# Two float products become PE transposes in the second layer of a graph network

## The chip, the cores and the metric

The kernel runs on one core of a Trainium2 chip. The metric is the device time of one execution in microseconds (us); lower is better. Before the change it is 5334.88 us, the median of three runs (5333.9 to 5344.31).

A core has five engines, each with its own queue that it works through in order: TensorE (PE, matrix products; its weight loads are listed apart as PEld), VectorE (DVE), ScalarE (ACT), GpSimd (POOL) and SyncE (SP, which only issues transfers here). They wait for each other by semaphores.

## The reference

Two layers of a graph network with 12,500 nodes, 200,000 edges sorted by destination, 64 features and 8 edge types, each layer followed by a residual and a layer norm. The change lies in the second one:

```python
Z = jnp.einsum('ni,rio->nro', h, fc_weight)
z_s = Z[src, etype]
z_d = Z[dst, etype]
aw = attn_weight[etype, :, 0]
e = jax.nn.relu(jnp.sum(jnp.concatenate([z_s, z_d], axis=1) * aw, axis=1))
m = jax.ops.segment_max(e, dst, num_segments=N)
ex = jnp.exp(e - m[dst])
denom = jax.ops.segment_sum(ex, dst, num_segments=N)
h_out = jax.ops.segment_sum((ex / denom[dst])[:, None] * z_s, dst, num_segments=N)
```

So it is a softmax over the edges that enter a node: a score per edge, the maximum over each destination's edges, the exponential of the difference, and a weighted sum.

## The kernel before

Edges are taken in runs of 512 (four chunks of 128), and two runs make a group: 391 runs, 196 groups. The edges being sorted, the destinations of a run fall into a window of W = 96 nodes. Work on a window is done with one-hot matrices: `oh` (edges by window places) and `ohT` (the other way round).

The second layer's function `sum1` handles one group. It is a Python generator that is cut into pieces by `yield`. The loop that calls it interleaves pieces of up to five groups in a fixed order, written out by hand (`group(i + 3)`, `node(i)`, `group(i)` and so on), and every engine's queue is filled in that order. The function `finish1` does the same for the nodes that are complete, from group 90 on. Going through `sum1`:

- Loads: SP brings `row` (L507) and `dw` (L606); POOL gathers the rows `zg` of the table of Z by eight indirect transfers a group (L95), into one of five buffers.
- `ps_row` (PE, L615) spreads the destinations' places over 96 partitions, ACT makes `ohT` of it (L616, L619), and PE looks up the destination's part of the score (`pq`, L624).
- DVE builds `oh` (L361), the scores (L630 to L640), and the largest score of each lane for each window place, `t` (L648 to L652).
- PE turns `t` with a transpose into `tt` (L658, tile pt), so that the window's places lie on partitions. DVE reduces it to one maximum a place, `m` (L663).
- L665: `m` lies on partitions and is wanted along the free axis, on all C = 65 partitions. It is a product with `m`, broadcast to 65 columns, as the stationary operand and the unit matrix as the moving one. The result is `rows`.
- DVE takes the larger of that and of the running maxima `top` (`most`, L673), and the difference `d` (L674); ACT writes `top` back (L675).
- L683: one row of `most` is turned back, so that the places lie on partitions again: a product of that row as the stationary operand with a 1 by 1 tile that holds a one. The result is `column`, one column a run.
- DVE splits `column` into three bfloat16 parts `mq` (`parts`, L434 to L437), PE looks up each edge's maximum from them (`pm`, L690), and DVE subtracts it from the score (`em`, L694 and L695).
- ACT takes the exponentials (L696, L698) and weighs the gathered rows (`wz`, L700). PE adds them up by window (`sums`, L704), and DVE adds the sums to the accumulators `acc` (L708, L709).

In PE's queue a steady group's order is: L704 (8 products), L683 (2), L615, L624 (8), L615, the transpose of a finished node L724, L658 (2), L690 (8), L665 (2). In DVE's queue it is: m, em, acc, most and d, the scores, t, mq, oh, each for the group whose turn it is.

The first layer (`sum0`, `finish0`) has the same manner of queues. Its products are L407 and L422, and it is not touched by the change.

Of the kernel before, what the change touches and what calls it, by code (L numbers as in the profile page):

```python
# [53 lines left out]
W = 96  # L54
# [11 lines left out]
C = D + 1  # L66
# [4 lines left out]
def gnn_kernel(ctx: ExitStack, tc, x, xT, xP, src, dstp, dst, et, eaT, u, W1, b1, W2, b2, fc, aw, out):  # L71
    nc = tc.nc
# [40 lines left out]
    with (  # L113
# [35 lines left out]
        ident = consts.tile([128, 128], F32, name="ident")  # L149
# [22 lines left out]
        one_f = consts.tile([1, 1], F32, name="one_f")  # L172
# [429 lines left out]
    def sum1(work, psum, n, chunks, idx, rel_of, et_of, row_of, wins_of, odd=0):  # L602
# [19 lines left out]
        for k in range(n * KS):  # L622
            s, i = divmod(k, KS)
# [32 lines left out]
        rows = pt[:C, n * EC:].rearrange("p (s w) -> p s w", s=n)  # L656
# [5 lines left out]
        m = work.tile([W, n], F32, name="m")  # L662
        nc.vector.tensor_reduce(m, tt, AX.X, OP.max)  # L663
        for s in range(n):
            nc.tensor.matmul(rows[:, s, :], m[:, s:s + 1].to_broadcast([W, C]), ident[:W, :W],  # L665
                             start=True, stop=True)
        yield

        most = work.tile([C, n, W], F32, name="most")
# [10 lines left out]
        column = pb[:W, 2 * n * W:2 * n * W + n]  # L680
        pm = pb[:, 2 * n * W + n:].rearrange("p (k j) -> p k j", j=3)
        for s in range(n):
            nc.tensor.matmul(column[:, s:s + 1], most[0:1, s, :], one_f, start=True, stop=True)  # L683
        yield
        mq = work.tile([W, n, 3], BF16, name="mq")
        parts(work, column, lambda i: mq[:, :, i], [W, n])
# [1 line left out]
        for k in range(n * KS):  # L688
            s, i = divmod(k, KS)
# [12 lines left out]
        for k in range(n * KS):  # L702
            s, i = divmod(k, KS)
# [48 lines left out]
    with (  # L752
# [14 lines left out]
        for i in range(-3, NG - 2):  # L767
            g = i + 3
            if g < NG:
                n, chunks, c = span(g)  # L770
                groups[g] = sum1(work, psum, n, chunks, row_i[:, c], rel[:, c], et_i[:, c],
                                 row_load(work, g), wins_load(g), g % 2)
# [53 lines left out]
    with tc.For_i(0, some):  # L826
# [21 lines left out]
        with (  # L848
            tc.tile_pool(name="r1", bufs=1) as work,
            tc.tile_pool(name="r1_ps", bufs=1, space=PSUM) as psum,  # L850
        ):
            acc, top = sums_of(work)

            def edges1(r, w):
                idx, rl, row, base = further(work, r, w)
                chunks = ds(r * KS, KS)
                etx = work.tile([EC, KS], I32, name="x_et")
                nc.vector.tensor_copy(etx, et_i[:, chunks])
                nc.vector.tensor_copy(idx, row_i[:, chunks])
                all_of(sum1(work, psum, 1, KS, idx, rl, etx, lambda: row, lambda engine: [base]))  # L860

            def node1(at):
                y = work.tile([P, 1, D], F32, name="y1")
                mv = work.tile([P, 1, nc.vector.BN_AGGR_DIM], F32, name="ln_mv")
                all_of(finish1(work, psum, lambda engine: at, lambda: (y[:, 0, :], mv[:, 0, :])))
                all_of(scale1(work, [at], y, mv))

            anew(edges1, node1)
# [45 lines left out]
```

## Time and profile before

| | us |
|---|---|
| median of three runs | 5334.88 |
| the profiled execution | 5314.15 |
| its span (first to last instruction) | 5312.4 |
| PE busy (matmuls) | 2942.6 (55%) |
| PE weight loads busy | 2299.9 (43%) |
| DVE busy | 2485.7 (47%) |
| ACT busy | 1445.6 (27%) |
| POOL busy | 2953.5 (56%) |

The profile is of one execution. An entry names the line, the engine, the operation, and the tiles as out<-in. In a table of groups there follow the count, the busy time in us, the mean time of one in ns, and the engine's idle time just before, with what ended it. The times at which matmuls end are modelled; when a result really arrived is seen from the instruction that waited for it. Busy times of an engine can overlap and say nothing on their own about what sets the end. The chain of waits goes back from the last instruction, at each step to what released it; where it finds no instruction that did, it says "another core or an unknown queue". The second layer fills the stretch from about 2640 us to the end.

### The profile page before, as it was taken

The page shows a single profiled execution, that of the slowest core. Times are in us where ns is not written, and L with a number is a line of the kernel's source. Part 1 is how long each engine was busy: PE and PEld are TensorE (multiplying, and loading weights), DVE is VectorE, ACT ScalarE, POOL GpSimd, SP SyncE. Part 2 cuts the span into 40 slices and gives each one's busy share as a digit, 9 for nine tenths or more (in the row PEclk, how much of TensorE's full clock was granted, in tenths as well). Part 3 has the DMA queues.
Part 4 walks back from the last instruction along what each step waited for, and adds up shares of the span by engine and source line. Part 5 has one row for each costly group of instructions (what it writes and reads, how often), then busy time and mean ns, then how long its engine had stood idle before and what let it go on. Part 6 is the DMA issues. An engine that isn't in the chain of part 4 may idle for free.

```text
span 5312.4 us, 62590 instructions
## 1 busy us (share of the span) xinstructions
PE 2942.6 (55%) x16633; PEld 2299.9 (43%) x16634; DVE 2485.7 (47%) x8113; ACT 1445.6 (27%) x3717; POOL 2953.5 (56%) x3140
## 2 busy tenths in 40 slices
PE   3455555555677777777454454445444455545454
PEld 2344444444555555555333333333333333333333
DVE  2022222222444444445455555555556556666566
ACT  1000000000111111111343343444444445444454
POOL 5466665566565565664255555555555555555553
PEclk6555555555556565656655555555555555555555
DMA  3121111111222222222111111111111111111111
GB/s 123 30 63 37 35 37 35 36 37 36 56 64 61 64 64 61 64 62 66 44 22 21 22 22 21 22 22 21 23 23 24 26 25 26 26 24 26 25 25 20
DMA packets 294054, 204.87 MB, mean 39 GB/s; under 512 B 214573, under 2 KB 214703, under 8 KB 293274
## 3 DMA queue, kind: packets, MB, share of 16 engines
q0 software_dynamic: 100032, 103.43, 9.8%
q1 hardware_dynamic: 189180, 87.46, 6.4%
q10 hardware_dynamic: 4480, 9.91, 0.6%
q8 instruction: 134, 2.20, 0.2%
q14 instruction: 228, 1.87, 0.1%
HBM read 158.55 MB, written 41.97 MB: 38 GB/s over the span
## 4 chain that ended last, share of the span: by engine, by line
another core or an unknown queue 32%; DVE 24%; PE 16%; issue 15%; ACT 9%; DVEq 2%; DMA 1%; POOL 0%; ACTq 0%; SPq 0%; POOLq 0%
PE pa L422 5%; ACT wz L700 4%; PE pm L407 3%; DVE oh L361 3%; DVEq L335 2%; PE pb L704 2%; DVE psc L648 2%; DVE oe L648 2%; DVE d L674 1%; DVE most L673 1%; PE pt L665 1%; DVE msg L416 1%; DVE t L651 1%; DVE psc L650 1%
## 5 line engine op out<-in xcount | busy, mean ns | idle before, releaser
L95 POOL DMA_INDIRECT zg<-z_tab,row_i x1563 | 1474.5, 943 | 1287.2 <-ACT top L675 641.5
L95 POOL DMA_INDIRECT bg<-b_tab,src_i x1523 | 1438.1, 944 | 1008.7 <-issue 398.4
L704 PE MATMUL pb<-oh,wz 128*65 128x96 f32 x3128 | 551.2, 368 | 553.7 <-ACT wz L700 304.4
L422 PE MATMUL pa<-oh,msg 128*64 128x96 f32 x3128 | 539.6, 364 | 574.3 <-ACT msg L417 441.4
L704 PEld LDWEIGHTS pb<-oh,wz 128*65 128x65 f32 x3128 | 494.6, 227 | 609.9 <-ACT wz L700 343.1
L422 PEld LDWEIGHTS pa<-oh,msg 128*64 128x64 f32 x3128 | 483.0, 222 | 600.7 <-ACT msg L417 454.2
L417 ACT ACTIVATE msg<-msg 128x512 f32<-128x512 f32 x191 | 120.0, 629 | 2089.5 <-DVE msg L416 1946.8
L407 PEld LDWEIGHTS pm<-aw,cb 128*128 128x128 f32 x3128 | 579.2, 284 | 135.8 <-issue 131.7
L407 PE MATMUL pm<-aw,cb 128*128 128x64 f32 x3128 | 618.6, 376 | 2.3 <-issue 2.3
L428 DVE TENSOR_TENSOR xa<-xa,pa 64x96 f32 x391 | 100.9, 258 | 817.7 <-remote 514.1
L416 DVE TENSOR_TENSOR msg<-pm,bg 128x512 f32<-128x512 f32 x191 | 131.4, 688 | 740.9 <-remote 608.8
L616 ACT ACTIVATE off<-ps_row,minus_p 96x512 bf16<-96x512 f32 x391 | 266.0, 680 | 553.4 <-remote 275.1
L615 PE MATMUL ps_row<-row,ones_row 1*96 1x512 bf16 x391 | 217.0, 555 | 340.6 <-ACT off L616 165.5
L700 ACT ACTIVATE wz<-zg,wz 128x64 f32<-128x64 f32 x1564 | 394.7, 335 | 6.4
L361 DVE TENSOR_TENSOR oh<-psc,rel 128x768 f32<-128x768 f32 x392 | 371.4, 948 | 7.0 <-DMA z_tab<-z 4.2
L665 PE MATMUL pt<-ident,m 96*65 96x96 f32 x782 | 176.5, 379 | 342.9 <-issue 145.9
L665 PEld LDWEIGHTS pt<-ident,m 96*65 96x65 f32 x782 | 119.5, 220 | 360.3 <-issue 151.5
L694 DVE TENSOR_REDUCE em<-pb 128x8 f32<-128x24 f32 x196 | 35.3, 180 | 509.9 <-remote 444.2
L696 ACT ACTIVATE pb<-d 65x192 f32<-65x192 f32 x196 | 64.2, 327 | 717.8 <-DVE em L694 443.0
L402 DVE TENSOR_SCALAR cb<-ps_row,iota_p 96x1024 f32<-96x1024 f32 x196 | 246.2, 1256 | 11.2 <-PE ps_row L355 7.2
L481 PE MATMUL pw<-wsd,x1T 64*125 64x16 f32 x212 | 60.9, 365 | 315.1 <-DVE y L454 314.5
L481 PEld LDWEIGHTS pw<-wsd,x1T 64*125 64x125 f32 x212 | 50.7, 295 | 377.1 <-DVE y L454 376.2
(151 smaller groups left out, 3982.0 us busy)
## 6 DMA issues: line engine op xcount, KB each, us to landing
z_tab<-z SPq DMA_DIRECT2D x106, 253.9 KB
zg<-z_tab,row_i POOLq DMA_INDIRECT x1563
cb<-in_eaT SPq DMA_DIRECT2D x195, 128.0 KB
bg<-b_tab,src_i POOLq DMA_INDIRECT x1523
aw<-a_tab SPq DMA_DIRECT2D x391, 24.0 KB
dw<-d_tab SPq DMA_DIRECT2D x391, 4.7 KB
row<-rel_tab SPq DMA_DIRECT2D x390, 2.0 KB
xn<-in_x SPq DMA_DIRECT2D x106, 31.2 KB
```

The costliest lines, as they stand in the source:

```text
L95: nc.gpsimd.indirect_dma_start(out=to[:, k, :], out_offset=None, in_=table[:, :], in_offset=bass.IndirectOffsetOnAxis(ap=idx[:, k:k + 1], ...
L361: nc.vector.tensor_tensor(oh, iota_n[:, None, :].to_broadcast([EC, n * KS, W]), rel_of.unsqueeze(2).to_broadcast([EC, n * KS, W]), OP.is_e ...
L402: nc.vector.tensor_scalar(cb[:W, :, :], ps_row, iota_p[:W], None, OP.is_equal)
L407: nc.tensor.matmul(pm[:, k, :], cb[:, s, i * EC:(i + 1) * EC], aw_t[:, s, :], start=True, stop=not raw)
L416: nc.vector.tensor_add(msg, pm, bg)
L422: nc.tensor.matmul(pa[D:, s, :], msg[:, k, :], oh[:, k, :], start=(i == 0), stop=(i == KS - 1))
L615: nc.tensor.matmul(ps_row[:, :RE], ones_row, row[:, s, :], start=True, stop=True)
L616: nc.scalar.activation(off[:, s, :], ps_row[:, :RE], AF.Abs, bias=minus_p[:W])
L648: nc.vector.tensor_mul(to, by_run[:, :, i, :], es[:, :, i].unsqueeze(3).to_broadcast([EC, n, half, W]))
L665: nc.tensor.matmul(rows[:, s, :], m[:, s:s + 1].to_broadcast([W, C]), ident[:W, :W], start=True, stop=True)
L700: nc.scalar.activation(wz[:, k, :D], zg[:, k, :D], AF.Copy, scale=wz[:, k, D:])
L704: nc.tensor.matmul(sums[:, s, :], wz[:, k, :], oh[:, k, :], start=(i == 0), stop=(i == KS - 1))
```

## The change

Two statements of `sum1` are changed. In both, the product of two float32 operands becomes the transpose operation of PE, with the same operands in the same roles: what is turned is the stationary operand, and the unit matrix (or the one) is the moving one. No instruction changes its place in a queue, and no buffer or loop is altered.

```diff
         for s in range(n):
-            nc.tensor.matmul(rows[:, s, :], m[:, s:s + 1].to_broadcast([W, C]), ident[:W, :W],
-                             start=True, stop=True)
+            nc.tensor.transpose(rows[:, s, :], m[:, s:s + 1].to_broadcast([W, C]), ident[:W, :W])
...
         for s in range(n):
-            nc.tensor.matmul(column[:, s:s + 1], most[0:1, s, :], one_f, start=True, stop=True)
+            nc.tensor.transpose(column[:, s:s + 1], most[0:1, s, :], one_f)
```

## The prediction

> **What bounds the kernel now.** The change touches the second layer alone, so I first looked at where that layer's time goes. The page's chain of waits comes first (shares of the span, by engine and by line).
>
> ```profile
> another core or an unknown queue 32%; DVE 24%; PE 16%; issue 15%; ACT 9%; DVEq 2%; DMA 1%; POOL 0%; ACTq 0%; SPq 0%; POOLq 0%
> PE pa L422 5%; ACT wz L700 4%; PE pm L407 3%; DVE oh L361 3%; DVEq L335 2%; PE pb L704 2%; DVE psc L648 2%; DVE oe L648 2%; DVE d L674 1%; DVE most L673 1%; PE pt L665 1%; DVE msg L416 1%; DVE t L651 1%; DVE psc L650 1%
> ```
>
> No engine carries the span. A third of the chain has no named owner, PE has 16% of it, and of the two lines that the change edits only L665 is listed, with 1%. The sums by stretch for the second layer (two windows, 2600 us; columns: length, then busy us of PE, PEld, DVE, ACT, POOL with their counts, then granted clock, DMA share, GB/s) show a stage bound by latency:
>
> ```profile
> 2640.00:3890.00 1250.00, 616.81 (x4114) 462.88 (x4115) 699.91 (x2439) 505.20 (x1405) 697.20 (x739) 0.54 0.12 22
> 3890.00:5240.00 1350.00, 668.95 (x4332) 502.97 (x4331) 812.29 (x3026) 644.11 (x1729) 729.18 (x773) 0.53 0.13 25
> ```
>
> DVE leads with 58% (1512 of 2600), PE has 49%. Taking the starts of L694 as the beat, the 196 groups come 13.3 us apart in the first 90 and 14.0 us apart while nodes are finished too. The last groups, for which nothing is gathered any more, show the beat that the same arithmetic can keep (timeline; columns: start, duration, engine, line, operation, tiles, and in brackets the idle time before):
>
> ```profile
> 5264.79 0.17 DVE L694 TENSOR_REDUCE em<-pb 128x8 f32<-128x24 f32 x1
> ...
> 5266.15 0.24 DVE L673 TENSOR_TENSOR most<-top,pt 65x96 f32<-65x96 f32 x1
> ...
> 5268.65 0.80 PE L683 MATMUL pb<-one_f,most 1*96 1x1 f32 x4
> ...
> 5273.71 0.17 DVE L694 TENSOR_REDUCE em<-pb 128x8 f32<-128x24 f32 x1
> ```
>
> From em to em: 8.92 us. There DVE has no idle time in front of m, em and most, and L683 comes as soon as DVE has made most. L665, started at 5264.92, is done at 5265.82, before most wants it. A group with gathers in flight looks different:
>
> ```profile
> 4050.09 0.40 PE L690 MATMUL pb<-mq,ohT 96*128 96x3 bf16 x8
> 4050.81 0.90 PE L665 MATMUL pt<-ident,m 96*65 96x96 f32 x4 [0.32 <-issue]
> ...
> 4052.43 0.18 DVE L694 TENSOR_REDUCE em<-pb 128x8 f32<-128x24 f32 x1 [1.67 <-PE pt L665]
> ...
> 4055.32 0.25 DVE L673 TENSOR_TENSOR most<-top,pt 65x96 f32<-65x96 f32 x1 [1.43 <-PE pb L704]
> ```
>
> em needs L690, whose drawn end is 4050.49, and starts 1.9 us after it; most needs L665, whose drawn end is 4051.71, and starts 3.6 us after it. So PE's results arrive later than drawn while POOL gathers, and this lateness (510 us of DVE idle before L694, 208 us before L663) is the bulk of the 32% without an owner. The page's names for it are not to be trusted: em doesn't read L665's result, and most doesn't read L704's.
>
> **The change part by part.** On every engine the order of instructions stays the same; only the kind of four matmuls in a group changes. The rows that price it:
>
> ```profile
> L665 PE MATMUL pt<-ident,m 96*65 96x96 f32 x782 | 176.5, 379 | 342.9 <-issue 145.9 <-DVE m L663 123.8 <-DVE oh L361 73.0
> L683 PE MATMUL pb<-one_f,most 1*96 1x1 f32 x782 | 151.8, 290 | 22.5 <-issue 10.8 <-DVE most L673 4.4 <-DVE ln_shift L746 2.2
> L658 PE MATMUL pt<-ident,t 128*96 128x128 f32 x391 | 117.7, 401 | 121.9 <-DVE mq L434 63.8 <-issue 37.1 <-DVE t L652 8.1
> ```
>
> There are 391 runs of edges, and each has one L665, one L683 and one L658. The float products leave 782 records, two for each product, with two weight loads; the transpose of L658 leaves 391, one each. That is the whole mechanism: a float product goes through the array in two recorded passes, a transpose in one.
>
> *Step 1, L665's size.* Four records take 0.90 us a group (176.5/196): the first about 0.42, each further one 0.16 later. Two take about 0.42 + 0.16 = 0.58, near the 0.60 (117.7/196) of L658, which is the larger shape. Saving 0.32 us.
>
> *Step 2, L683's size.* Four records take 0.775 us (151.8/196), so two take 0.29 + 0.17 = 0.46. Saving 0.32 us. Both together: 0.64 x 196 = 125 us of PE's time, 782 matmuls and 782 weight loads fewer. That is the ceiling if every bit lay on the path.
>
> *Step 3, what of L683 is on the path.* Its result is read by L434. In the group without gathers L683 ends at 5269.45 and L434 comes at 5271.86, with DVE busy between: 2.4 us of cover, by L630 to L652. Behind L683 in PE's queue stands L615, then ACT's L616 and L619, which feed a later group; 43 waits of ACT with 39.5 us are put down to L683. If that cover were gone it would cost 0.32 us a group, 63 us. I take 3 us: 0.41 (0.32 of 0.775) of the 6.4 us that the chain has on L683 in this layer.
>
> *Step 4, what of L665 is on the chain.* The chain has 59.9 us on L665 in this layer; 36% of it (0.32 of 0.90) is 21 us. Much of that was entered through em, which doesn't wait for L665, so the bounds are 0 and 21; I take 10.
>
> *Step 5, most waiting for L665.* The waits of L673 have
>
> ```profile
>   ACT top L675: 81.5, 101
>   PE pb L704: 50.7, 43
> ```
>
> The second line is, by the program, L665 arriving late. If L665 only becomes 0.32 us shorter, 43 x 0.32 = 14 us come back. If lateness goes by the number of PE's instructions (half as many, so half as late), nearly all 50.7 us go. I take 27, nearer to the lower end, because the one resource measured for sure is the shorter run. L704, queued behind L665 on PE, waits for wz of ACT (its first weight load idles 0.36 us for it in the group shown first), so a shorter L665 gives it nothing.
>
> *Step 6, the clock.* The Trainium skill ("TensorE: Matmul & The Clock Gate", Part 4: PE-mode transpose) says that transposes don't count as activity for the gate that raises TensorE's clock, which speaks against the change. The row: this layer is granted 0.54 and 0.53 of full speed, so it is at half speed for all but 6 to 8% of the time already. By the row the loss is nothing. By the rule, were all the full-speed stretches lost, some 7% of PE's 1286 us, 90 us, would run at half speed and take up to 90 us more of PE; at PE's 16% of the chain that is 14 us. I take 0 and keep 14 for the range.
>
> The sum against the profiled execution (5314.15 us, span 5312.4): -(3 + 10 + 27) = -40 us, 0.75%. The median of the runs shown, 5334.88, lies 20.7 us above the profiled one; I take the gain off the median: 5295.
>
> **The rivals.**
> *A. Everything is hidden.* DVE and the gathers set the beat; PE's shorter work becomes waiting. For it: the groups without gathers, where L665 and L683 have cover. Against: the waits in step 5. Time: 5325 to 5345.
>
> *B. Nearly all of PE's saving arrives.* PE is late for something that counts its instructions, about 92 a group of which 8 go. For it: 510 us of waits at L694, whose PE work is short. Against: these waits often end with the landing of the last gathered rows, which the change doesn't move. Time: 5334.9 - 125 = 5210, or a little above.
>
> *C. The beat locks to the gathers (slower).* A gather of eight chunks starts 3.0 us after em (em, then wz, frees the buffer); its rows are in 10.7 us later. Where em waits for that landing, the beat is 13.73 us and renews itself; now these groups mix with a pair of 11.6 and 14.9 us (mean 13.25), which has the late most of step 5 in it. If removing that lateness turns the pairs into locked groups, the first 90 groups go from 13.33 to 13.73: +36 us, 5371. It decides once over half the pairs lock and the gain elsewhere is below 18 us. Against: the second half, at 14.0, would gain from the same lock.
>
> *D. The pass count doesn't fall.* A stationary operand broadcast by a step of zero, or one partition high, could still be loaded twice. No row shows a transpose of either kind. Time as before.
>
> **How the numbers follow.** The difference that a measurement of this kernel can tell from none is about 0.2%, 11 us. The forecast (5265 to 5324): 0.47. B and what lies between: 0.15. A and D: 0.15. C, or the clock: 0.23. So faster 0.62, same 0.15, slower 0.23. The likeliest case's own range is 5265 to 5324. For 8 in 10 the range runs from 5218 (most of B) to 5362 (most of C).
>
> **What the changed profile would show.** Steps 1, 2: 391 records each at the two transposes, with about 0.58 and 0.46 us a group; if 782 remain, D holds. Step 3: L434 without a new wait. Steps 4, 5: L673's 50.7 us put down to L704 falls to 37 or below; near zero speaks for B. Step 6: the granted clock stays above 0.52. Rival A: the idle time of PE before L704 and L658 grows by what PE saves and the beat stays. Rival C: more beats at 13.7, fewer at 11.6 and 14.9. The prediction is wrong if PE's lateness under the gathers has a cause that the transposes change in either direction, since 700 us of waiting hang on it and I price only 27 of them.

## The result and the profile after

The changed kernel takes 5381.12 us (median; 5367.93 to 5388.14) where the kernel before takes 5334.39 (5332.63 to 5344.31): the ratio is 1.0074, 95% interval 1.0059 to 1.0089. It is 0.74% slower, 47 us, where 40 us of gain were forecast. In the changed kernel every line from L665 on is one lower than before: the transposes are L665 and L682, most is L672, em is L693.

The two edits did on PE what the diff says. From the groups by line of the changed kernel (busy us and mean ns after the first bar, idle time before and what ended it after the second):

```profile
L665 PE MATMUL pt<-ident,m 96*65 96x96 f32 x391 | 113.9, 394 | 390.7 <-DVE m L663 215.1 <-issue 98.4 <-DVE oh L361 77.0
L682 PE MATMUL pb<-one_f,most 1*96 1x1 f32 x391 | 65.0, 224 | 11.6 <-DVE most L672 5.9 <-DVE ln_st L732 1.9 <-DVE acc L708 1.8
```

Each transpose is one record, not two. Over 196 groups that is 0.58 us a group at L665 (0.90 before) and 0.33 at L682 (0.775 before). PE is busy for 2802.0 us instead of 2942.6. The sums by stretch for the second layer show the saving, and that the granted clock is what it was:

```profile
2640.00:3890.00 1250.00, 526.85 (x3626) 380.85 (x3626) 680.19 (x2360) 485.28 (x1359) 680.52 (x722) 0.54 0.13 21
3890.00:5240.00 1350.00, 588.90 (x3897) 424.10 (x3898) 798.59 (x2986) 634.18 (x1709) 716.86 (x760) 0.53 0.15 25
```

DVE's busy time in the same stretches fell from 1512 to 1479 us: fewer groups were done in them. The chain of waits of the changed kernel:

```profile
another core or an unknown queue 38%; DVE 22%; PE 14%; ACT 11%; issue 10%; DVEq 2%; DMA 0%; POOL 0%; ACTq 0%; POOLq 0%
```

PE fell from 16% to 14%, and the part without a named owner rose from 32% to 38%. Of the second layer alone it took 20.8% before (556 us) and 27.8% after (757 us), so 201 us; the rest of the rise lies in the first layer, which the change doesn't touch and which grew by only 3 us. The waits show where the second layer's part sits most. Before, ACT's L616 (it turns PE's broadcast row, L615, into the one-hot ohT that every later product of the group uses) waited 52 times for "remote", the view's word for an end of a wait to which it finds no instruction (us in total, times, longest):

```profile
ACT off L616 <- remote: 275.1, 52, 23.1
```

After:

```profile
ACT off L616 <- remote: 591.8, 122, 22.4
```

DVE's mq (L434), which reads the transposed column, did the same, first before and then after:

```profile
L434 DVE CAST mq<-pb 96x2 bf16<-96x2 f32 x195 | 29.5, 151 | 66.5 <-remote 66.5
L434 DVE CAST mq<-pb 96x2 bf16<-96x2 f32 x195 | 29.9, 153 | 172.0 <-remote 167.0 <-issue 4.8
```

DVE's m (L663) waits for 317.1 us instead of 236.4; in return em waits less, 360.5 instead of 509.9. All idle time of DVE from the first em on grows from 1096 to 1148 us, which is about the loss.

Two timelines show how. First the kernel before, one of its commonest groups (start, duration, engine, line, operation, tiles, idle time before; only the lines that matter, with the first gather of the batch, L616 and em). From here on, the gathers of an L616 or an em are the batch started last before it. By the program these are rows for a later group, the fourth after em's own:

```profile
3134.66 0.94 POOL L95 DMA_INDIRECT zg<-z_tab,row_i  x1 [4.01 <-ACT top L675]
...
3136.53 0.68 ACT L616 ACTIVATE off<-ps_row,minus_p 96x512 bf16<-96x512 f32 x1 [1.05 <-PE pb L683]
...
3143.39 0.94 POOL L95 DMA_INDIRECT zg<-z_tab,row_i  x1 [0.30 <-issue]
...
3144.68 0.18 DVE L694 TENSOR_REDUCE em<-pb 128x8 f32<-128x24 f32 x1 [3.95 <-remote]
```

L616 comes 1.87 us after the gathers start, em 10.02 us after it. The em before it was at 3131.65, so this beat is 13.03 us, and POOL had rested 4.01 us. Now the changed kernel, two groups in a row:

```profile
3112.55 0.94 POOL L95 DMA_INDIRECT zg<-z_tab,row_i  x1 [5.16 <-ACT top L674]
...
3114.28 0.68 ACT L616 ACTIVATE off<-ps_row,minus_p 96x512 bf16<-96x512 f32 x1 [0.90 <-PE ps_row L615]
...
3121.21 0.18 DVE L693 TENSOR_REDUCE em<-pb 128x8 f32<-128x24 f32 x1 [2.59 <-remote]
3121.29 0.94 POOL L95 DMA_INDIRECT zg<-z_tab,row_i  x1 [0.30 <-issue]
...
3124.21 0.94 POOL L95 DMA_INDIRECT zg<-z_tab,row_i  x1 [1.98 <-ACT top L674]
...
3125.27 0.64 PE L615 MATMUL ps_row<-row,ones_row 1*96 1x512 bf16 x1
...
3131.48 0.68 ACT L616 ACTIVATE off<-ps_row,minus_p 96x512 bf16<-96x512 f32 x1 [6.44 <-remote]
...
3136.24 0.17 DVE L693 TENSOR_REDUCE em<-pb 128x8 f32<-128x24 f32 x1
```

In the first group em comes 8.66 us after the gathers start, while the last gather has not even been issued. That beat is short, 11.65 us (the em before it was at 3109.56). The next batch follows 3.00 us after em as always, so POOL rests only 1.98 us. Then L615, drawn as finished at 3125.91, reaches ACT 5.57 us late, mq comes late too, and the beat is 15.03 us. The lateness is not ACT's: in the trace PE's semaphore rises at 3131.46, and L616 starts 0.02 us after that, as it does in the median of its 83 waits of over 4 us. The pair averages 13.34 us, and all 56 pairs of the changed kernel that begin with em at +8.6 average 13.48; in the kernel before, a group with em at +9.3 to +10.7 and the one after it averaged 13.0 to 13.2.

Counted over groups 8 to 186 (179 groups): em lay 9.3 to 10.7 us behind its gathers in 93 groups before and in 5 after, at 8.6 us in 19 before and 56 after, and near 11.5 us in 53 before and 95 after. The mean beat of the first 90 groups went from 13.34 to 13.70 us, that of the next 97 from 14.00 to 14.18: 90 x 0.36 + 97 x 0.18, about 50 us, of the 53.8 us between the two spans (5312.4 and 5366.2). The first em alone comes 3 us later.

### The profile page after: what moved, and what is told of

Read it like the earlier page. It is cut to its first block, busy times and chain, and to the rows that moved or that the text cites. A ratio compares the mean times of both kernels' runs of the same rounds, so it can differ in the third digit from the quotient of the medians.

```text
span 5366.2 us, 61026 instructions
## 1 busy us (share of the span) xinstructions
PE 2802.0 (52%) x15851; PEld 2158.9 (40%) x15852; DVE 2483.5 (46%) x8113; ACT 1441.1 (27%) x3717; POOL 2953.2 (55%) x3140
## 3 DMA queue, kind: packets, MB, share of 16 engines
q0 software_dynamic: 100032, 103.43, 11.3%
q14 instruction: 228, 1.87, 0.1%
## 4 chain that ended last, share of the span: by engine, by line
another core or an unknown queue 38%; DVE 22%; PE 14%; ACT 11%; issue 10%; DVEq 2%; DMA 0%; POOL 0%; ACTq 0%; POOLq 0%
PE pa L422 6%; ACT wz L699 5%; PE pm L407 3%; DVE oh L361 3%; DVE psc L648 2%; DVE oe L648 2%; DVEq L335 2%; DVE msg L416 1%; DVE psc L650 1%; ACT off L616 1%; DVE d L673 1%; DVE t L651 1%; DVE ed L633 1%; DVE most L672 1%
## 5 line engine op out<-in xcount | busy, mean ns | idle before, releaser
L615 PE MATMUL ps_row<-row,ones_row 1*96 1x512 bf16 x391 | 221.2, 566 | 547.4 <-ACT off L616 252.5
L616 ACT ACTIVATE off<-ps_row,minus_p 96x512 bf16<-96x512 f32 x391 | 266.3, 681 | 794.3 <-remote 591.8
L665 PE MATMUL pt<-ident,m 96*65 96x96 f32 x391 | 113.9, 394 | 390.7 <-DVE m L663 215.1
L658 PEld LDWEIGHTS pt<-ident,t 128*96 128x96 f32 x391 | 50.8, 181 | 446.1 <-issue 425.4
L663 DVE TENSOR_REDUCE m<-pt 96x2 f32<-96x256 f32 x196 | 81.3, 415 | 317.1 <-remote 287.5
L665 PEld LDWEIGHTS pt<-ident,m 96*65 96x65 f32 x391 | 57.4, 208 | 408.1 <-DVE m L663 222.2
L695 ACT ACTIVATE pb<-d 65x192 f32<-65x192 f32 x196 | 63.4, 323 | 556.9 <-DVE em L693 339.2
```

The lines of the kernel that those rows point to most:

```text
L615: nc.tensor.matmul(ps_row[:, :RE], ones_row, row[:, s, :], start=True, stop=True)
L616: nc.scalar.activation(off[:, s, :], ps_row[:, :RE], AF.Abs, bias=minus_p[:W])
L665: nc.tensor.transpose(rows[:, s, :], m[:, s:s + 1].to_broadcast([W, C]), ident[:W, :W])
```

## The experiments

The 18 runs met different chips, and the kernel before takes 5330 to 5354 us on three of them (like the chip of the result) and 3964 to 3972 on the other six, so each ratio below is against the kernel before on the same chip.

### The halves, on a chip where the kernel before takes 3967 us

Each half of the change alone; both halves with each transpose issued twice (as many records as the products had); and the changed kernel with a sixth buffer for the gathered rows.

```diff
# only_column
-            nc.tensor.matmul(column[:, s:s + 1], most[0:1, s, :], one_f, start=True, stop=True)
+            nc.tensor.transpose(column[:, s:s + 1], most[0:1, s, :], one_f)
# only_rows
-            nc.tensor.matmul(rows[:, s, :], m[:, s:s + 1].to_broadcast([W, C]), ident[:W, :W],
-                             start=True, stop=True)
+            nc.tensor.transpose(rows[:, s, :], m[:, s:s + 1].to_broadcast([W, C]), ident[:W, :W])
# twice: the changed kernel, and
+            nc.tensor.transpose(rows[:, s, :], m[:, s:s + 1].to_broadcast([W, C]), ident[:W, :W])
+            nc.tensor.transpose(column[:, s:s + 1], most[0:1, s, :], one_f)
# after_six: the changed kernel, and
-        zg = work.tile([EC, n * KS, C], F32, name="zg", bufs=5)
+        zg = work.tile([EC, n * KS, C], F32, name="zg", bufs=6)
```

> Only the product with the one (column) becomes a transpose; the product with the unit matrix (rows) stays. Theory 1 (place of em): PE works slowly while rows are gathered, and em comes as soon as PE has done pm; four PE instructions fewer ahead of pm bring em one step earlier, ahead of the landing of the gather; then the products L704 run under the next gather and the next beat is long. The column's product stands ahead of pm, so this alone gives most of the loss: 5360 to 5385 us, with beats of 11.6 and 14.9 us in turn. Theory 2 (a transpose itself disturbs PE, or takes longer than drawn): each transpose brings its share, so about half of the loss, 5350 to 5365, with beats of all lengths lengthened.

> Only the product with the unit matrix (rows) becomes a transpose; the product with the one (column) stays. Theory 1: the rows stand behind pm in PE's queue, so em doesn't come earlier by it; what stands behind it, L704, does: the time is that of before or a little shorter, 5310 to 5340 us. Theory 2: about half of the loss, 5350 to 5365 us.

> Both are transposes, and each is issued twice into the same place, so that PE has as many records as before (four for a group at each line). Theory 1: what counts is PE's work between the gathers, not its kind, so this brings the time of before back: 5325 to 5345 us, with beats of 13.0 and 13.7 us again. Theory 2: twice as many transposes, twice the loss: 5400 to 5430 us.

> The changed kernel with six buffers for the gathered rows in place of five. Theory 1: a gather then starts at once after the one before it, or earlier against em than 3.0 us, so the tie between em and the gather's start is gone and the beats of 11.6 and 14.9 in turn with it; how fast depends on how slow PE is under gathers without a break: between 12.0 and 14.0 us a group, 5000 to 5400 us, and below the changed kernel. Theory 2: as slow as the changed kernel, 5365 to 5390 us.

Measured: 3966.82, 3967.01, 3967.1 and 3966.4 us; ratios 1.0 (0.9991 to 1.0009), 1.0 (0.9992 to 1.0009), 1.0002 (0.9993 to 1.0011) and 0.9999 (0.9991 to 1.0008). Nothing moves. The expectations were written for the other kind of chip and all miss. The chain of only_column says why:

```profile
POOL 50%; issue 21%; DMA 15%; DVE 9%; ACT 2%; PE 2%; DVEq 1%; ACTq 0%; POOLq 0%; SPq 0%
```

Here POOL's gathers, issued back to back, set a beat of 9.9 to 10.0 us, there is no chain part without an owner, and ACT's L616 waits for PE by name:

```profile
L616 ACT ACTIVATE off<-ps_row,minus_p 96x512 bf16<-96x512 f32 x391 | 265.7, 680 | 205.6 <-PE ps_row L615 205.2
```

The changed kernel itself on another chip of this kind:

> The changed kernel itself, beside the kernel before. In the runs of the two halves on another chip, the kernel before took 3966.9 us and not 5334, and none of four variants differed from it by more than 0.02%; there no register instruction of SP took 0.7 us, while 217 of 1419 did in the first trace. Theory 3 (the chip): the 0.7% belongs to chips on which PE and SP work slowly while rows are gathered; on a chip without that, POOL's gathers set the beat at 10.0 us and the change is hidden: ratio 0.999 to 1.001, 3963 to 3970 us. On a chip with it: ratio 1.005 to 1.010, 5365 to 5390 us. Theory 2 (a transpose itself costs): ratio above 1.003 on either.

Measured: 3967.52 against 3968.57 us, ratio 0.9997 (0.9988 to 1.0006). So the 0.74% is a matter of the chips where PE's results arrive late under the gathers, and on the others the change is worth nothing either way.

### More work on PE

Both kernels with the products of L704 computed three times over, to put PE on the path:

```diff
-        for k in range(n * KS):
+        for k in 3 * [*range(n * KS)]:
```

> The kernel before, with the products L704 of a group carried out three times (the first two results are overwritten), so that PE has 5.6 us more to do in a group and sets the beat. From the row of L704 (551 us for 196 groups, 2.8 us a group): beat 12.5 to 14.5 us in place of 10.0, 4450 to 4850 us where the kernel before takes 3967. It is the base of the next run.

> The changed kernel with the products tripled in the same way. It prices the change where PE sets the beat. If a transpose is worth the pass that it saves (the prediction's steps 1 and 2: 0.32 us each, of which the rows' share may hide behind wz): 60 to 125 us less than the tripled kernel before, ratio 0.973 to 0.988. If transposes cost PE more than their records show (theory 2): no gain, or a loss.

Measured, again where the kernel before takes 3964 us: 4033.05 (ratio 1.0172, 1.0155 to 1.0189) and 4028.28 (1.0161, 1.0144 to 1.0178). 6256 further matmul records (twice L704's 3128) cost 1.7%, with beats of 10.2 us in both, and the transposes give back 4.8 us of it. The expectation missed: PE's load is hardly on the path there even so.

### em tied to the landing of its gathers

A copy of the newest batch's last column ahead of em makes em wait until that batch has landed, in both kernels.

```diff
+    newest = []
         gather(zg, z_tab, idx, chunks)
+        newest.append(zg)
 ...
+        tie = work.tile([EC, 1], F32, name="tie")
+        nc.vector.tensor_copy(tie, newest[-1][:, newest[-1].shape[1] - 1, :1])
         em = work.tile([EC, n * KS], F32, name="em")
```

> The kernel before with one more DVE instruction ahead of em: it copies one column of the rows that were asked for last, so em waits for the landing of the newest gather. This puts in by hand what the first trace shows (em coming no earlier than that landing). If the loop em, wz, buffer free, gather, landing, em is what sets a beat of 13.7 us, then the beat here is 3.0 + 10.7 = 13.7 us plus the copy: 13.7 to 14.0 us, 4650 to 4750 us. If the gathers set their own pace whatever em does, the beat stays at 10.0 us and the time at 3967 to 3990.

> The changed kernel with the same tie. In a loop held by the landing, PE's 0.64 us a group lie beside the gather: within 0.2% of the tied kernel before. A difference of +0.7% here would say that the tie to the landing alone makes the loss.

> The tied kernel before with six buffers for the gathered rows: the gather then waits for the products of one group earlier, and the loop spans two beats. If the loop was the cause, the beat falls to POOL's own 10.0 us, 3967 to 4000 us; if not, it stays with the tied kernel before.

Measured where the kernel before takes 5338.08 us: before_tied 5452.45 (1.0225, 1.0183 to 1.0267), after_tied 5447.3 (ratio 1.0218 to the kernel before), so 0.9991 between the two medians. In both, em lies at +11.3 us in the median and beats are 14.3 to 14.5 us; POOL always rests more than 3 us, and L616 is late in 46 of 179 groups of each. With em's place fixed, the change no longer loses. The level, 14.3 instead of the expected 13.7 to 14.0, was missed.

before_tied_six, with the sixth buffer on top, took 5333.62 us (1.0002, 0.9984 to 1.002), neither of the two cases expected: there em lay at +8.6 to +12 as in the kernel before, so the tie did not bind. Its trace shows why:

```profile
3110.50 0.14 DVE L697 COPY tie<-zg 128x1 f32<-128x1 f32 x1
...
3114.54 0.18 DVE L699 TENSOR_REDUCE em<-pb 128x8 f32<-128x24 f32 x1 [3.91 <-remote]
```

With six buffers the batch in flight is that of the fifth group after em's, not of the fourth; the tile that the tie reads is the batch before it and has landed, so the copy waits for nothing and em comes 4.04 us after it. The gathers still start 3.00 us after an em, and the time is that of five buffers.

### The halves again, where the kernel before takes 5330 us

> Only the last step (the product with a one, L683) is a transpose. Theory (em earlier: with four records fewer between the most and the gates, em falls at +8.6 us after its batch's gathers start instead of at +9.3 to +10.7, the products then run under gathers, and beats come in pairs of about 12 and 14.9): 5355 to 5385 us where the kernel before takes 5335, and more than 50 of 179 groups at +8.6. Rival (the loss comes from the transposes of m, L665): 5325 to 5340. On a chip where the kernel before takes 3967: 3964 to 3970 by both.

> Only the transposes of m (L665) are changed. Theory (em earlier): two thirds of the saved PE time but none of it between the most and the gates; m's rows come 0.32 us earlier, so em moves too if the most does not wait for anything else: 5320 to 5365 where the kernel before takes 5335, less loss than only_column. Rival (the loss comes from these transposes): 5360 to 5390. On a chip where the kernel before takes 3967: 3964 to 3970 by both.

> Both steps are transposes, each issued twice, so PE has as many matmul records as before. Theory (the time of em decides, not the kind of operation): the records of the products are back, so the loss is gone: 5320 to 5350 where the kernel before takes 5335, with the groups at +9.3 to +10.7 back (70 or more of 179). Rival (the transpose as an operation costs something behind it): 5365 to 5395. On a chip where the kernel before takes 3967: 3964 to 3970 by both.

Measured, against 5329.57 us on the same chip: only_column 5386.7 (1.0101, 1.0063 to 1.0139), only_rows 5315.26 (0.9973, 0.9960 to 0.9985), twice 5348.38 (1.0024, 1.0007 to 1.0042). The parts add up: +57 and -14 make +43, and the whole change measured +47. The transposed column brings the entire loss; the transposed rows bring a gain. The column's time lies just above its range, with 49 groups at +8.6 and not more than 50; that of the rows lies below its range.

ACT's L616 in the groups by line separates the two. The column alone:

```profile
L616 ACT ACTIVATE off<-ps_row,minus_p 96x512 bf16<-96x512 f32 x391 | 266.7, 682 | 738.1 <-remote 534.7 <-PE ps_row L615 99.7 <-issue 39.2
```

The rows alone, nearly as before (553.4, remote 275.1):

```profile
L616 ACT ACTIVATE off<-ps_row,minus_p 96x512 bf16<-96x512 f32 x391 | 266.1, 681 | 577.7 <-remote 302.5 <-PE ps_row L615 134.1 <-issue 60.4
```

The program's order explains the difference. L615 stands directly behind the column's matmuls in PE's queue, so they are what it waits for. With two matmul records and two weight loads fewer there, L616 comes 1.72 us after the gathers' start in the groups where it is prompt, instead of 2.20. Behind the rows' transposes stand the products of L704, which wait for wz; with the rows alone L616 stays at 2.20 us.

The run with doubled transposes puts the count of PE's records back to 16633, the number of the kernel before, and still loses 0.24%. So it is not the count alone, though with the count back most of the loss is gone; and a cost that each transpose brought with it would have grown, since there are twice as many. Its four transposes of the column are through earlier than the four passes of two products (the last starts 1.13 us after the gathers' start, not 1.37): L616 comes at 1.88 us, between the two kernels, and the time lies between them too. Of its expectation the theory's time came true and the classes did not: only 30 groups, not 70, lie at +9.3 to +10.7.

### A longer rest for POOL

By then I held that a rest of POOL under about 2.1 us between two batches causes the late L616. Lengthening the rest should then cure the changed kernel. POOL fills zg once or twice ahead of the gathers, which overwrite it.

```diff
+        for _ in range(2):                      # after_rest: once
+            nc.gpsimd.memset(zg, 0.0)
         gather(zg, z_tab, idx, chunks)
```

> The changed kernel with two fills of zg on POOL ahead of each group's eight gathers (no work of the reference; they fill rows that the gathers overwrite): by the one-buffer fill of 171 ns for 65 columns against 101 for one, about 0.6 us each for 520, so the gathers start some 1.3 us later after the gates. Theory (a rest of POOL under about 2.1 us between two batches of gathers makes the next group's row values, L616, late every time, and beats of 12 and 14.9 alternate): the rest after a short beat grows from 1.9 to about 3.2 us, the late L616 after short beats are gone, beats go to about 13 to 13.3 in the first half, and the time falls below both kernels: 5200 to 5320 where the kernel before takes 5335. Rival (the pairs come from something else, and gathers are only later): every beat grows by up to 1.3 us, 5400 to 5600. On a chip where the kernel before takes 3967, POOL bounds the beat and the fills add up to 1.3 us to each of 190: 3990 to 4220 by both.

> The same with one fill of zg, some 0.6 us: the rest of POOL after a short beat grows from 1.9 to about 2.6 us. Theory: between the two cases, since at rests of 2.1 to 3 us 11 of 28 groups of the kernel before were late: 5280 to 5370 where the kernel before takes 5335. Rival: 5390 to 5490. On a chip where the kernel before takes 3967: 3970 to 4090 by both.

Measured against 5354.23 us: two fills 5562.93 (1.0395, 1.0369 to 1.0422), one fill 5490.84 (1.0267, 1.0238 to 1.0297). The times are those of the rival (the second 1 us above its range), and the cure failed. But the rival's uniformly longer beats are not what the trace shows. With two fills (timeline; the fills are L609, L615 has become L617, L616 L618 and em L695):

```profile
3119.48 1.12 POOL L609 MEMSET zg<- 128x520 f32 x2 [6.60 <-ACT wz L701]
...
3120.87 0.95 POOL L95 DMA_INDIRECT zg<-z_tab,row_i  x1 [0.27 <-POOL zg L609]
...
3125.90 0.18 DVE L695 TENSOR_REDUCE em<-pb 128x8 f32<-128x24 f32 x1
...
3130.00 0.64 PE L617 MATMUL ps_row<-row,ones_row 1*96 1x512 bf16 x1
...
3131.97 0.95 POOL L95 DMA_INDIRECT zg<-z_tab,row_i  x1 [0.27 <-POOL zg L609]
...
3143.87 0.68 ACT L618 ACTIVATE off<-ps_row,minus_p 96x512 bf16<-96x512 f32 x1 [13.93 <-remote]
...
3146.15 0.17 DVE L695 TENSOR_REDUCE em<-pb 128x8 f32<-128x24 f32 x1
```

The gathers started later, but em moved from +8.6 to +5.0 us behind them, by more than the fills took. So the rest did not grow, beats became 9.8 and 20.3 us, and the alternation got larger. My mistake was to hold em's distance from the gathers fixed.

The times alone can't tell more: 190 starts that come 0.6 or 1.2 us later would be 114 and 228 us if each were simply added, and the measured ratios lie 1.9% and 3.2%, about 103 and 171 us, above the changed kernel's. The pattern does, in one table over all kernels of this kind of chip:

| kernel | ratio | L616 after the gathers' start, where prompt | groups after a rest under 2.1 us, all with L616 late | L616 waiting for "remote", us |
|---|---|---|---|---|
| before | 1 | 2.20 | 23 | 275.1 |
| only_rows_b | 0.9973 | 2.20 | 23 | 302.5 |
| twice_b | 1.0024 | 1.88 | 57 | 568.0 |
| only_column_b | 1.0101 | 1.72 | 66 | 534.7 |
| changed kernel | 1.0074 | 1.72 | 66 | 591.8 |
| after_rest | 1.0267 | 1.13 | 69 | 808.4 |
| after_rest_two | 1.0395 | 0.54 | 88 | 1184.2 |

Down the table PE's work starts sooner behind the gathers; with that come more short rests and, but for one row, more waiting of L616. The waiting does not give the time by itself: twice_b has nearly that of the changed kernel and a third of its loss, and only_rows_b has more than the kernel before and is faster. (In the last two rows the fills' own delay is part of the ratio, and a fill is counted as rest.) The fourth column is a count without exception: in all 392 such groups of the seven traces L616 came later than 2.6 us behind the gathers' start. If only POOL's idle time is taken as rest, 7 groups of after_rest are exceptions. After longer rests L616 was late in 36 of 156 groups before and in 6 of 113 after.

### The gathers moved, without any transpose

If the place of PE's work against the gathers is the cause, then starting the gathers about half a microsecond later in the kernel before must give the changed kernel's loss.

```diff
+        nc.gpsimd.memset(zg[:, :3 * n, :], 0.0)
         gather(zg, z_tab, idx, chunks)
```

> The kernel before, all products as they are, with one fill of six of zg's eight column blocks on POOL ahead of each group's gathers (no work of the reference). One whole fill took 0.536 us and moved L616's start from 1.69 to 1.09 us after the gathers' start (0.60), so this one should move the gathers some 0.49 us later against PE's work: as far as the transposed column moves PE's work earlier against the gathers (L616 at 2.16 us before, 1.69 after). Theory (what costs is the place of PE's work against the gathers, from whichever side it is moved): the time of the changed kernel, 5365 to 5400 where the kernel before takes 5335, em at +8.6 us in more than 45 of 179 groups, at +9.3 to +10.7 in fewer than 30. Rival (the transposes themselves, or the gathers' later start as such, 190 times 0.49 us): without that change of classes, 5335 or 5425. On a chip where the kernel before takes 3967: 3967 to 4070 by both.

> The same kernel once more, for a chip where the kernel before takes 5335 us. Theory (the place of PE's work against the gathers costs, from whichever side it is moved): 5365 to 5400, em at +8.6 us in more than 45 of 179 groups and at +9.3 to +10.7 in fewer than 30. Rival (the transposes themselves, or the later start as such): 5335, or 5425 by 190 times 0.49 us, without that change of classes. On a chip where the kernel before takes 3967: 4050 to 4060, as measured.

> Last try of the same kernel for a chip where the kernel before takes 5335 us. Theory (the place of PE's work against the gathers costs, from whichever side it is moved): 5365 to 5400, em at +8.6 us in more than 45 of 179 groups and at +9.3 to +10.7 in fewer than 30. Rival (the transposes themselves, or the later start as such): 5335, or 5425 by 190 times 0.49 us, without that change of classes. On a chip where the kernel before takes 3967: 4045 to 4060, as measured twice.

All three met chips where the kernel before takes 3964 to 3972 us, and gave 4055.54, 4048.24 and 4048.46 us (ratios 1.0212, 1.0214, 1.0212). There POOL sets the beat and each of about 190 fills of 0.44 us is simply added, 84 us. They say nothing on the question, which stays open where it matters.

## Why the prediction was wrong

**The step that failed is step 3.** It priced the shorter column (L683) at a gain of 3 us, since DVE's work covers the column's own reader, and said of what is behind it in PE's queue only that L615, then L616 and L619, "feed a later group". The column alone measured +57 us. What moved was that queue: where prompt, L616 came 0.48 us earlier against the gathers; em, mostly at +9.3 to +10.7 before, came by turns at +8.6 and near +11.5; and after an em at +8.6 the next batch of gathers, which em sets going, found POOL rested for 2 us only. The step also expected L434 "without a new wait"; L434's wait grew from 66.5 to 172.0 us.

**Step 1 held, and step 2 was sized too small.** 0.58 us a group was forecast at L665 and measured; at L683 0.46 was forecast and 0.33 measured: a transpose takes 224 ns where a pass took 290, and the second adds 0.10 us instead of 0.16. About 141 us left PE's busy time, more than the ceiling of 125, and none of it reached the end.

**Steps 4 and 5 had the right sign and too large a size.** Together they gave 37 us; the rows alone gave 14. Step 5 watched the most's waits put down to L704. These hardly moved, 48.6 us with the rows alone and 54.2 in the changed kernel against 50.7 before, and that the lateness goes with the number of PE's instructions is not seen. The most's idle time as a whole did fall, by 24.3 us, near step 5's 27; the kernel before first, then the rows alone:

```profile
L673 DVE TENSOR_TENSOR most<-top,pt 65x96 f32<-65x96 f32 x391 | 97.4, 249 | 160.6 <-ACT top L675 81.5 <-PE pb L704 50.7 <-remote 9.8
L672 DVE TENSOR_TENSOR most<-top,pt 65x96 f32<-65x96 f32 x391 | 97.4, 249 | 136.3 <-ACT top L674 84.3 <-PE pb L703 48.6 <-PE pt L665 1.2
```

But in that trace em waits 14.6 us longer and m 21.7. The profiled execution of the rows alone, 5326.49 us, lies near the top of its runs and above that of the kernel before, 5314.15, so where the 14 us come from can't be read from it and stays open.

**Step 6 held.** The granted clock stayed 0.54 and 0.53. The remark of the Trainium skill that transposes don't count for the clock gate ("TensorE: Matmul & The Clock Gate", Part 4: PE-mode transpose) cost nothing here.

**The rivals.** C had the sign and almost the time, 5371, but the opposite mechanism, so its number is luck: it feared that pairs of 11.6 and 14.9 us would lock at 13.73. The beats near 13.7 vanished (40 before, none after), and pairs of about 12 and 14.9 took their place. A holds on the other kind of chip and for the rows' step in part. B and D are refuted by the sizes above. The prediction also read the waits at L694 and L663 as the bulk of the 32% without an owner. They can't be: 32% of the span is 1700 us, and only 556 us of it lie in the second layer. The prediction named the danger in its last sentence, that 700 us of waiting hang on PE's lateness while only 27 were priced; it gave that no price, though the trace of before already held both regimes. Its 19 groups with em at +8.6 us were followed by beats of 15.6 us on average, and its 23 rests under 2.1 us were each followed by a late L616. Sorting the groups of that trace by em's distance from the gathers would have shown that earlier is worse, and later too: the beats that end and follow such an em average 13.7 us at +8.6, 13.0 to 13.2 at +9.3 to +10.7, and 14.2 at +11.5.

**What is shown and what is argued.** That the column's step carries the loss and the rows' step does not is shown by the halves. That a short rest of POOL is followed by a late L616 is a count over seven traces, not a test: the attempt to lengthen the rest failed, and the test that moves the gathers without a transpose ran only where the kernel before takes 3964 to 3972 us. The tied pair agrees that the loss goes with em's place. So the path from the column's step to the loss, by em's place and POOL's rest, is argued from traces and not shown by a test. Why results that PE is drawn to have finished reach ACT and DVE up to 13 us late while gathers are in flight, and why 0.48 us on PE moves em by 1 to 2, no run tells.

Of all kernels tried, only_rows is the one that beats both: 0.27% faster than before where the kernel before takes 5330 us, and equal to it (1.0, 0.9992 to 1.0009) where it takes 3967.

## What to carry to other kernels

When an edit shortens a step that is well covered, price what stands behind it in its engine's queue, and ask against which transfer of another engine that work now runs. In a loop whose transfers are started by its own results, earlier can be slower: sort the groups of the trace of before by how far their result lies behind the transfers' start, and read the beats around each. Measure the halves of a change apart, since +57 and -14 look like one small loss.

## What the hardware showed that I had not expected

- The same kernel takes 5330 to 5354 us on some chips and 3964 to 3972 on others, 1.34 times. The gathers cost POOL 944 ns each on both. What differs as far as the traces show is when PE's results arrive: ACT's L616 waited 275 us for a "remote" releaser in the trace of the kernel before at 5314 us, and at most 1 us for anything but L615 in the two single-edit runs at 3967 us.
- On the first kind em's distances from its gathers' start stand in steps of about 0.7 us (8.6, 9.3, 10.0, 10.7). One kind of SP's register instructions (FUSED_REGOPS) there took 0.6 to 0.8 us in 217 of 1419 cases in the kernel before, and in none of 1419 on a chip of the second kind. That the two belong together is not shown.
- Two transposes of one float row each take 0.33 us where two float products took 0.775, so the pass count halves and the passes get shorter too, 224 instead of 290 ns in the mean.
